# Jobs get TensorE in even steps and VectorE in odd ones, and the scans lie 138 steps behind the attention

## The chip, the cores and the metric

The kernel runs on one core of one Trainium2 chip. Its time is the device time of one execution in microseconds (us); the time given for a kernel is the median of its runs. A core has five engines with queues of their own: TensorE (PE in the profile; PEld is its loading of weights), VectorE (DVE), ScalarE (ACT), GpSimd (POOL) and SyncE (SP), which here only issues DMAs. TensorE writes its results into PSUM[...].

## The reference

Two layers in sequence, on x of 4 images x 128 channels x 64 x 64, all in float32. The first is attention over the 4096 positions of an image, with four heads of 32 channels, a residual and a layer norm:

```python
Q = split_heads(x_flat @ Wq + bq)      # and K, V alike
attn = softmax(einsum('bhnd,bhmd->bhnm', Q, K) * scale, axis=-1)
out = einsum('bhnm,bhmd->bhnd', attn, V)
y = out @ Wo + bo + x_flat
y = layernorm(y) * gamma + beta
```

The second is a sum of three branches on its output:

```python
spatial = conv_3x3(x) + conv_spatial_b
spectral = irfft2(conv_1x1(rfft2(x)))
xi, z = split(u @ in_proj)                   # u: x as 4096 rows; 2 x 256 channels
xs = silu(causal_conv_4_taps(xi))
dt, Bm, Cm = split(xs @ x_proj)              # 8, 16, 16 columns
dt = softplus(dt @ dt_proj + dt_proj_b)
h = exp(dt * A) * h + dt * Bm * xs           # per position; 16 states per channel
y = sum(h * Cm) + xs * D
ym = (y * silu(z)) @ out_proj
return spatial + spectral + ym
```

## The kernel before

**Tiling.** The 4 x 4096 positions are cut into 32 chunks of 512 (`L`), eight per image (`NCH`). The heads are taken in two pairs (`PAIRS`), so a chunk of queries has two halves, 64 in all (`HALVES`). A half goes over the 4096 keys in 32 blocks of 128 (`NT`). One block for one half is a step; a chunk takes 64 steps (`SLOT`), and the attention takes 2,048 steps, counted by `t` from 0. Keys and values of one image stay in SBUF; while one image is worked on, those of the next are projected, one chunk in each period of 64 steps.

**One step.** Nothing is scheduled by a compiler: the loop in lines 1059 to 1107 writes the instructions in the order in which each engine runs them. In a step it issues

- `scores_for_exp(H, m)` (L486): six matmuls (L494) into the PSUM tile "s2", four of queries against keys and two that subtract each query's maximum (`MX`); ACT takes the exponential (L502).
- `scores_for_max`, seven steps ahead (`LEAD`): four matmuls (L454) into the PSUM tile "s1", of which DVE takes the maximum (L461).
- the scans of an earlier chunk. At `LAG` = 144 steps behind the attention each chunk has 2 x 16 pairs of channel half and state, each taking two steps. Even steps issue `scan_state` (L834): the scan itself on DVE (L844), a copy of the last column (L853) and the product with C (L854) on POOL, and the accumulation (L871, L873) on POOL. Odd steps issue `scan_decay` (L827, ACT, into PSUM "dA"), `scan_input_term` (L832, POOL) and, where a buffer is free, `scan_load` (L810 or L816), which SP issues.
- the jobs, by `plan.step` (below).
- `times_values` (L505): four matmuls (L514) that multiply the exponentials with the values. After the last block of a half, the result is copied out of PSUM in two parts, by ACT (L524) and DVE (L525).

"s1", "s2" and "dA" have one buffer each: the matmuls that write one wait until its reader is done.

**Jobs.** All other work is written as generators, `Job`s, in a `Plan` (L84 to L158). A job yields what its next piece needs: "P" for TensorE, "D" for VectorE, "A" for ScalarE, "B" for one of two PSUM banks, "" for nothing but the next step. `plan.step(t, places)` goes over the open jobs by rank, start time and age, and advances each of them whose needs the step's places hold; a place is used up by each advance. After its first advance a job goes on in the same step only over yields that are just "P" (late: "P", "A" or "D") and have a place; any other yield waits for a later step. POOL instructions and DMAs need no place: they are issued with the piece that they stand in. A job that can't have what it needs waits for a later step, and so do its followers.

The main loop hands out places by step (L1093 to L1104): before the attention's first steps all engines; in the attention, odd steps `{"D": 2, "P": 2, "A": 2}` and even ones `{"D": 0, "P": 0, "A": 1}`, so TensorE and VectorE jobs go into odd steps only; after the attention (`plan.late`) only odd steps, with `{"D": 4, "P": 4, "A": 6}`.

**The jobs in question**, with their start lines L1030 to L1057:

- keys and values of a chunk of the next image: `project_kv` (matmuls L350, L364; DVE L355; ACT L376), queries: `project_q` (L417).
- `maxima` (L463): four DVE operations (L467 to L471) form the maxima of the coming half, TensorE transposes them (L476), ACT copies them out as `MX` (L482), which `scores_for_exp` of that half reads.
- `normalise` (L529), for each finished half: SP stores the sums of the exponentials (L541) and the values (L543), reloads the sums in another layout (L546), DVE takes the reciprocal (L549), SP stores it (L551) and reloads it spread over the rows (L554), POOL multiplies (L558). Then `output_projection` (L567): matmul L573, residual L576 on DVE, transposes L580, layer-norm statistics L587 to L593 on DVE, their logarithm and exponential on ACT (L595, L596), small products on POOL (L598 to L601), normalising on DVE (L610).
- `mamba_input` (L644) and `scan_input` (L683) for each half of the channels: matmuls L661 and L687, the four taps on DVE (L697, L702), a sigmoid (ACT L626 to L636 with one DVE piece, L634), its product on POOL (L712). `scan_bc` (L718) follows with two matmuls (L724), and `scan_dt` (L738; matmul L742, ACT L748 to L760, POOL L765 to L767, ACT L774).
- `gate` (L777; matmul L783, a sigmoid, POOL L791), `spectral` (L887; L893, L903, L905), `convolve` (L917; nine matmuls L928 and one L933, ACT L938), `scan_output` (L961; the gate's product, matmuls L995, DVE L999, flipped rows on POOL, L958 and L959), `flips` (L1007), which finishes chunks of an image's first half once the flipped rows are there.

**After the attention.** The last chunk's scans end well over a hundred steps behind its attention; in them the accumulation goes to TensorE (L880, `add_states`, four steps after the scan) instead of POOL, in four buffers taken from the values' space. The two score tiles, and the values' PSUM tile, are used again there.

Of the kernel before, what the change touches and what calls it, by code (L numbers as in the profile page):

```python
# [17 lines left out]
P = 128  # L18
# [143 lines left out]
def attention_then_conv_mamba(  # L162
# [164 lines left out]
    plan = Plan(2, {"x": 2, "f": 1})  # L327
# [114 lines left out]
    def scores_for_max(H, s):  # L442

        k = H % PAIRS
        m, t = divmod(s, TPC)
        assert have["K", k, m] == H // PAIRS // NCH
        if s == 0:
            part[H] = att.tile([P, TPC, 2, NCH], F32, tag="part", name=f"part_{H}")

        tag = "s2" if H == 0 and s % 2 else "s1"  # L450
        sc = psum.tile([P, 2, L], F32, tag=tag, name=f"s1_{H}_{s}")
        for n in range(2):
            for j in range(2):
                nc.tensor.matmul(  # L454
                    sc[:, j, :],
                    QT[H][rows[j], n, t * P : (t + 1) * P],
                    KK[k][m][rows[j], :],
                    start=n == 0,
                    stop=n == 1,
                )  # L460
        nc.vector.tensor_reduce(part[H][:, t, :, m], sc, AX.X, ALU.max)  # L461
# [24 lines left out]
    def scores_for_exp(H, m):  # L486

        k = H % PAIRS
        i, t = divmod(m, TPC)
        assert have["K", k, i] == H // PAIRS // NCH  # L490
        s = psum.tile([P, 2, L], F32, tag="s2", name=f"s2_{H}_{m}")
        for n, mov in enumerate((QT[H][:, 0, :], QT[H][:, 1, :], MX[H])):
            for j in range(2):
                nc.tensor.matmul(  # L494
                    s[:, j, :],
                    sel[rows[j], :] if n == 2 else KK[k][i][rows[j], t * P : (t + 1) * P],
                    mov[rows[j], :],
                    start=n == 0,
                    stop=n == 2,
                )  # L500
        e = att.tile([P, 2, L], F32, tag="e", name=f"e_{H}_{m}", bufs=3)
        nc.scalar.activation(e, s, AF.Exp)  # L502
        es[H, m] = e
# [273 lines left out]
    def gate(c):  # L777

        gates[c] = [None, None]
        for hf in range(NH):  # L780
            bank = yield "PB"
            pz = bank_tile(bank, [P, RPC, W], f"pz_{c}_{hf}")
            nc.tensor.matmul(  # L783
                pz, inw[:, DI + hf * P : DI + (hf + 1) * P], inner(c), start=True, stop=True
            )
            yield "A"
            plan.release(bank)
            z = loc.tile([P, L], F32, tag=f"zg{hf}", name=f"zg_{c}_{hf}", bufs=1)
            nc.scalar.activation(z, pz.rearrange("p r w -> p (r w)"), AF.Identity)
            a = yield from sigmoid(z, "sgz", f"{c}_z{hf}")  # L790
            nc.gpsimd.tensor_tensor(z, z, a, ALU.mult)  # L791
            gates[c][hf] = z
# [28 lines left out]
    def scan_decay(c, v):  # L821
        n, hf = divmod(v, NH)
        k = hf * NS + n

        tag = "o" if plan.t >= HALVES * NT + 2 and v % 2 else "dA"
        dA[c, v] = psum.tile([P, L], F32, tag=tag, name=f"dA_{c}_{k}")
        nc.scalar.activation(dA[c, v], dts[c][hf], AF.Exp, scale=negA[:, k : k + 1])  # L827
# [89 lines left out]
    def convolve(c):  # L917

        i = c % NCH
        while c not in edges or c not in hxs:  # L920
            yield ""
        bank = yield "PB"
        pf = bank_tile(bank, [P, RPC, W], f"pf_{c}")
        for k in range(9):
            if k:
                yield "P"
            dy, dx = divmod(k, 3)
            nc.tensor.matmul(  # L928
                pf, cw[:, k, :], xps[c][:, dy : dy + RPC, dx : dx + W], start=k == 0, stop=False
            )  # L930
        flat = pf.rearrange("p r w -> p (r w)")
        yield "P"
        nc.tensor.matmul(flat, g_hil, hxs.pop(c), start=False, stop=True)  # L933
        yield "A"
        plan.release(bank)
        ym = loc.tile([P, L], F32, tag="ym", name=f"ym_{c}", bufs=2)
        yms[c] = ym
        nc.scalar.activation(ym, flat, AF.Identity, bias=col("conv_b"))  # L938
        if i == 0:
            nc.gpsimd.tensor_tensor(ym[:, :W], ym[:, :W], sbias, ALU.add)  # L940
# [20 lines left out]
    def scan_output(c):  # L961

        b, i = divmod(c, NCH)
        late = i < NCH // 2
        yield "f"
        while not all(gates[c]) or c not in yms:
            yield ""

        for hf in range(NH):
            if c in sums_late:  # L970
                total = sums_late[c][:, hf, :]
                if (c, hf) in accs:
                    nc.vector.tensor_tensor(accs[c, hf], accs[c, hf], total, ALU.add)
                    total = accs[c, hf]
                else:
                    accs[c, hf] = loc.tile([P, L], F32, tag=f"acc{hf}", name=f"acc_{c}_{hf}")
                nc.vector.tensor_tensor(accs[c, hf], total, gates[c][hf], ALU.mult)
            else:
                nc.gpsimd.tensor_tensor(accs[c, hf], accs[c, hf], gates[c][hf], ALU.mult)
        if not late:  # L980
            wr = load_flipped(c)
        for _ in range(3):
            yield ""
        bank = yield "PB"
        pf = bank_tile(bank, [P, L], f"py1_{c}")
        for hf in range(NH):
            if hf:
                yield "P"
            nc.tensor.matmul(
                pf, outw[:, hf, :], accs[c, hf], start=hf == 0, stop=hf == NH - 1  # L990
            )
        yield "D"
        plan.release(bank, 2)
        ob = loc.tile([P, L], F32, tag="ob", name=f"ob_{c}", bufs=1)
        nc.vector.tensor_tensor(ob, yms.pop(c), pf, ALU.add)  # L995
        if late:
            yield ""
            ymd[c] = dram.tile([P, L], F32, tag="ymd", name=f"ymd_{c}", bufs=NCH)
            nc.sync.dma_start(ymd[c], ob)  # L999
        else:  # L1000
            add_flipped(ob, wr)
            yield ""
            yield ""
            nc.sync.dma_start(out[b, :, i * L : (i + 1) * L], ob)
        plan.places["f"] += 1
# [19 lines left out]

    LEAD = 7
    SLOT = PAIRS * NT
    LAG = 2 * SLOT + 16
    STATES = NH * NS
    for b in range(B):  # L1030

# [16 lines left out]
    for c in range(CHUNKS):  # L1048
# [3 lines left out]
        plan.at(t0 + SLOT + 30, 3, convolve(c))  # L1052
        plan.at(c * SLOT + LAG + 6, 3, gate(c))
        plan.at((c + 1) * SLOT + LAG + (2 if c < CHUNKS - 3 else 6), 0, scan_output(c))
    for b in range(B):
# [3 lines left out]
    t = 6 - SLOT  # L1059
    loaded = 0  # L1060
    end = (CHUNKS + 3) * SLOT
    while t < end or not plan.idle():
        H, m = divmod(t, NT)
        if 0 <= H < HALVES:
            scores_for_exp(H, m)
        h1, s1 = divmod(t + LEAD, NT)
        if 0 <= h1 + 1 < HALVES:
            scores_for_max(h1 + 1, s1)
        H, m = divmod(t - 1, NT)
        last = m == NT - 1  # L1070
        if last and 0 <= H < HALVES:
            times_values(H, m)
        c, s = divmod(t - LAG, SLOT)
        odd = s % 2 == 1
        if -1 <= c < CHUNKS:
            v = c * STATES + s // 2
            if not odd:
                if v >= 0:
                    scan_state(*divmod(v, STATES))
            else:  # L1080
                if 0 <= v + 1 < CHUNKS * STATES:
                    scan_decay(*divmod(v + 1, STATES))
                if 0 <= v + 2 < CHUNKS * STATES:
                    late = t > HALVES * NT
                    scan_input_term(
                        *divmod(v + 2, STATES), nc.vector if late else nc.gpsimd
                    )

                if loaded < CHUNKS * NS and loaded // NS in bcds:
                    if ring[0] or spare and spare[0][0] <= t:  # L1090
                        scan_load(*divmod(loaded, NS))
                        loaded += 1
        plan.late = t > HALVES * NT  # L1093
        if plan.late:
            add_states()
            if odd:
                plan.step(t, {"D": 4, "P": 4, "A": 6})
            plan.t = t
        elif t < -LEAD:
            plan.step(t, {"D": 4, "P": 4, "A": 4})  # L1100
        elif odd:
            plan.step(t, {"D": 2, "P": 2, "A": 2})
        else:
            plan.step(t, {"D": 0, "P": 0, "A": 1})  # L1104
        if not last and 0 <= H < HALVES:
            times_values(H, m)
        t += 1
# [76 lines left out]
```

## Time and the profile before

| what | value |
|---|---|
| median of 3 runs | 6037.3 us (6036.54 to 6038.84) |
| profiled execution, own time | 6038.33 us |
| its span | 6036.5 us |
| TensorE clock granted, mean | 0.987 |
| maxima L461: DVE, 2048 times | mean 1221 ns |
| exponentials L502: ACT, 2048 times | mean 1023 ns |
| scans L844, with a state carried in: DVE, 826 times | mean 1275 ns |
| products L854, POOL, 948 times | mean 1277 ns |
| input terms L832, POOL, 948 times | mean 1282 ns |
| accumulations L873, POOL, 894 times | mean 1281 ns |

The span is the part of the execution from the first to the last recorded instruction. A line of the page's groups has: line, engine, operation, output<-inputs, partitions x elements, count; then busy time and the mean of one in ns; then the idle time of the engine just before such instructions and what ended most of it. A line of the waits view has: the waiting group <- what released it, then the sum of the waits in us, their count, and the longest. A line of the timeline has: start and duration in us, engine, line, operation, output<-inputs, sizes and number of equal instructions in a row, and in brackets the idle time before it with its releaser. Where the text says "opening", it means the first matmuls L494 of a step.

### The profile page before, as it was taken

How to read it: one execution, taken by the hardware profiler on the slowest of the kernel's cores; microseconds unless marked ns; L12 is line 12 of the kernel's file. 1: busy time of each engine (PE TensorE's matmuls, PEld its weight loads, DVE VectorE, ACT ScalarE, POOL GpSimd, SP SyncE). 2: the span in 40 equal slices, each digit the busy share in tenths (PEclk: the TensorE clock that was granted, in tenths of full speed). 3: DMA queues.
4: the chain of work that ended last, by engine and by line, in shares of the span. 5: the costliest groups of instructions: out<-in, count | busy, mean ns of one | idle time of the engine just before them, and what ended most of it. 6: DMA issues, size and time to landing. Idle time of an engine off the chain costs nothing. (4 is left out here: it accounts for less than half of the span.)

```text
span 6036.5 us, 82731 instructions
## 1 busy us (share of the span) xinstructions
PE 5847.1 (97%) x31382; PEld 2443.1 (40%) x31382; DVE 4360.0 (72%) x4569; ACT 3586.6 (59%) x4826; POOL 4482.6 (74%) x4522
## 2 busy tenths in 40 slices
PE   5999999999999999999999999999999999999976
PEld 2444444444444444444444444444444444444422
DVE  4557777777777777777777777777777777777657
ACT  1455666666666666666666666666666666666653
POOL 0006888778887778888788888777888887888877
PEclk7999999999999999999999999999999999999988
DMA  4012222224333223223432222322433222222233
GB/s 125 25 36 58 65 71 75 71 70 110 82 89 73 73 72 74 72 64 89 104 84 82 74 68 71 75 68 73 108 75 92 67 67 63 66 71 63 62 98 89
DMA packets 266641, 455.28 MB, mean 75 GB/s; under 512 B 46688, under 2 KB 48256, under 8 KB 266240
## 3 DMA queue, kind: packets, MB, share of 16 engines
q1 hardware_dynamic: 261584, 448.11, 28.1%
q8 instruction: 246, 4.03, 0.3%
q10 hardware_dynamic: 4656, 1.87, 0.1%
q14 instruction: 155, 1.27, 0.1%
HBM read 375.68 MB, written 65.80 MB: 73 GB/s over the span
## 5 line engine op out<-in xcount | busy, mean ns | idle before, releaser
L461 DVE TENSOR_REDUCE part<-s 128x2 f32<-128x1024 f32 x2048 | 2498.1, 1221 | 1411.4 <-PE s L454 1407.6
L502 ACT ACTIVATE e<-s 128x1024 f32<-128x1024 f32 x2048 | 2095.5, 1023 | 2121.6 <-PE s L494 2117.0
L514 PE MATMUL po<-e,V 128*33 128x512 f32 x8192 | 2180.9, 605 | 2.4 <-DVE oz L525 0.3
L494 PE MATMUL s<-Q,K 64*128 64x512 f32 x8192 | 1501.0, 444 | 13.5 <-ACT e L502 10.2
L454 PE MATMUL s<-K,Q 64*128 64x512 f32 x8192 | 1308.9, 397 | 41.4 <-DVE part L461 32.3
L854 POOL TENSOR_TENSOR hs<-hs,bc 128x512 f32<-128x512 f32 x948 | 1211.0, 1277 | 170.3 <-DVE hs L844 101.3
L494 PEld LDWEIGHTS s<-Q,K 64*128 64x128 f32 x8192 | 610.2, 185 | 1736.3 <-ACT e L502 1237.0
L832 POOL TENSOR_TENSOR db<-u,bc 128x512 f32<-128x512 f32 x948 | 1215.6, 1282 | 0.0
L873 POOL TENSOR_TENSOR acc<-acc,hs 128x512 f32<-128x512 f32 x894 | 1145.4, 1281 | 70.1
L844 DVE TENSOR_TENSOR_SCAN hs<-dA,state,db 128x512 f32<-128x512 f32 x826 | 1052.8, 1275 | 41.9 <-ACT dA L827 40.1
L454 PEld LDWEIGHTS s<-K,Q 64*128 64x128 f32 x8192 | 750.1, 185 | 294.9 <-DVE part L461 129.4
L494 PE MATMUL s<-MX,sel 64*128 64x512 f32 x4096 | 808.0, 391 | 0.0
L827 ACT ACTIVATE dA<-dt,negA 128x512 f32<-128x512 f32 x1024 | 703.2, 687 | 115.7 <-DVE V L844 69.5
L853 POOL COPY state<-hs 128x1 f32<-128x1 f32 x858 | 157.9, 184 | 789.8 <-DVE hs L844 786.0
L514 PEld LDWEIGHTS po<-e,V 128*33 128x33 f32 x8192 | 305.4, 109 | 886.5 <-issue 840.8
L494 PEld LDWEIGHTS s<-MX,sel 64*128 64x128 f32 x4096 | 383.9, 185 | 90.7
L928 PE MATMUL pf<-xp,cw 128*128 128x512 f32 x576 | 288.2, 618 | 0.0
L558 POOL TENSOR_TENSOR op<-op,rz 128x512 f32<-128x512 f32 x32 | 41.4, 1294 | 178.6 <-DMA rz<-rd 175.8
L844 DVE TENSOR_TENSOR_SCAN hs<-dA,zero,db 128x512 f32<-128x512 f32 x128 | 163.2, 1275 | 0.9 <-POOL db L832 0.7
L880 PE MATMUL acc<-V,cst 128*128 128x512 f32 x140 | 95.0, 783 | 63.6 <-POOL V L854 63.5
L928 PEld LDWEIGHTS pf<-xp,cw 128*128 128x128 f32 x576 | 96.8, 189 | 119.6 <-issue 117.9
L712 POOL TENSOR_TENSOR xs<-xs,sg_x 128x512 f32<-128x512 f32 x64 | 81.8, 1279 | 79.3 <-ACT sg_x L636 79.3
(147 smaller groups left out, 3571.2 us busy)
## 6 DMA issues: line engine op xcount, KB each, us to landing
bc<-bcd SPq DMA_DIRECT2D x487, 512.0 KB
Q<-qd SPq DMA_DIRECT2D x256, 128.0 KB
K<-kd SPq DMA_DIRECT2D x64, 256.0 KB
K<-bcd SPq DMA_DIRECT2D x42, 256.0 KB
vd<-vst SPq DMA_DIRECT2D x32, 264.0 KB
V<-vd SPq DMA_DIRECT2D x32, 264.0 KB
xq<-in_x SPq DMA_DIRECT2D x32, 256.0 KB
xk<-in_x SPq DMA_DIRECT2D x32, 256.0 KB
```

The source lines that it names most:

```text
L454: nc.tensor.matmul(sc[:, j, :], QT[H][rows[j], n, t * P : (t + 1) * P], KK[k][m][rows[j], :], start=n == 0, stop=n == 1,)
L461: nc.vector.tensor_reduce(part[H][:, t, :, m], sc, AX.X, ALU.max)
L494: nc.tensor.matmul(s[:, j, :], sel[rows[j], :] if n == 2 else KK[k][i][rows[j], t * P : (t + 1) * P], mov[rows[j], :], start=n == 0, stop= ...
L502: nc.scalar.activation(e, s, AF.Exp)
L514: nc.tensor.matmul(po[H][used[j], :], VA[i][:, t, 2 * k + j, :], e[:, j, :], start=m == 0, stop=m == NT - 1,)
L827: nc.scalar.activation(dA[c, v], dts[c][hf], AF.Exp, scale=negA[:, k : k + 1])
L832: engine.tensor_tensor(db[c, v], us[c][hf], bcs[c, n][0], ALU.mult)
L844: nc.vector.tensor_tensor_scan(hs, dA.pop((c, v)), db.pop((c, v)), state[:, k : k + 1] if c % NCH else zero, ALU.mult, ALU.add,)
L853: nc.gpsimd.tensor_copy(state[:, k : k + 1], hs[:, L - 1 :])
L854: nc.gpsimd.tensor_tensor(hs, hs, bcs[c, n][1], ALU.mult)
L873: nc.gpsimd.tensor_tensor(accs[c, hf], accs[c, hf], hs, ALU.add)
L928: nc.tensor.matmul(pf, cw[:, k, :], xps[c][:, dy : dy + RPC, dx : dx + W], start=k == 0, stop=False)
```

## The change

Two things are changed. `LAG` goes from 144 to 138, so that everything that is placed by it comes six steps earlier against the attention: the scans of every chunk with their loads, decays and input terms, and the start times of `gate` and `scan_output`. And the places for jobs are split by step. In the attention, odd steps keep two for VectorE and two for ScalarE and lose TensorE's two, which go to the even steps. After the attention, VectorE's four stay in odd steps, TensorE's four go to even steps, and ScalarE's six are three in each. `plan.t = t` after `plan.step` in the late part goes too: since `plan.step` is now called in every step and sets it, it is set after `add_states` instead of in every step by a line of its own. The places before the attention's first steps stay.

```diff
@@ -1025,7 +1025,7 @@
     LEAD = 7
     SLOT = PAIRS * NT
-    LAG = 2 * SLOT + 16
+    LAG = 2 * SLOT + 10
@@ -1094,14 +1094,15 @@
         if plan.late:
             add_states()
             if odd:
-                plan.step(t, {"D": 4, "P": 4, "A": 6})
-            plan.t = t
+                plan.step(t, {"D": 4, "P": 0, "A": 3})
+            else:
+                plan.step(t, {"D": 0, "P": 4, "A": 3})
         elif t < -LEAD:
             plan.step(t, {"D": 4, "P": 4, "A": 4})
         elif odd:
-            plan.step(t, {"D": 2, "P": 2, "A": 2})
+            plan.step(t, {"D": 2, "P": 0, "A": 2})
         else:
-            plan.step(t, {"D": 0, "P": 0, "A": 1})
+            plan.step(t, {"D": 0, "P": 2, "A": 1})
```

## The prediction

> **What bounds the kernel now.** I read the page first, then the waits of TensorE, then the timeline of one period and of the end. The chain that ended last holds only the final 5 us and says nothing here. From the page:
>
> ```profile
> PE 5847.1 (97%) x31382; PEld 2443.1 (40%) x31382; DVE 4360.0 (72%) x4569; ACT 3586.6 (59%) x4826; POOL 4482.6 (74%) x4522
> PE   5999999999999999999999999999999999999976
> POOL 0006888778887778888788888777888887888877
> ```
>
> TensorE is busy in every slice but the first and the last two, so the run has two parts: the attention, bound by TensorE, up to about 5813 us, and an end of some 220 us in which it isn't. In the timeline each step opens with the first scores matmuls for the exponential; here are three openings in a row:
>
> ```profile
> 5689.86 0.73 PE L494 MATMUL s<-Q,K 64*128 64x512 f32 x4
> ...
> 5692.20 0.73 PE L494 MATMUL s<-Q,K 64*128 64x512 f32 x4
> ...
> 5694.54 0.73 PE L494 MATMUL s<-Q,K 64*128 64x512 f32 x4
> ```
>
> A step without anything else takes 2.344 us, and of the 2,048 openings most stand exactly so far apart, or that plus the TensorE job in the step. No plan can shorten these, only the stalls. The waits view names them:
>
> ```profile
> PE acc L880 <- POOL V L854: 63.5, 38, 14.9
> ...
> PE s L454 <- DVE part L461: 32.3, 62, 1.5
> ...
> PE s L494 <- ACT e L502: 10.2, 44, 1.4
> ```
>
> The first is in the end; the other two, 42.5 us, are most of what the attention loses. The scores' two PSUM tiles have one buffer each, so a late maximum (DVE) or exponential (ACT) stops TensorE. The largest recurs once in each 64-step period:
>
> ```profile
> 2516.91 0.69 DVE L525 COPY oz<-po 33x512 f32<-33x512 f32 x1 [0.38 <-ACT oz L524]
> ...
> 2517.64 1.28 DVE L844 TENSOR_TENSOR_SCAN hs<-dA,state,db 128x512 f32<-128x512 f32 x1
> ...
> 2518.84 1.20 DVE L461 TENSOR_REDUCE part<-s 128x2 f32<-128x1024 f32 x1
> ...
> 2520.09 0.73 PE L454 MATMUL s<-K,Q 64*128 64x512 f32 x4 [0.47 <-DVE part L461]
> ```
>
> The copy of a finished half and a scan come before the maximum, and TensorE waits. The start-to-start spacings in this view give effective costs: exponential 0.92, decay 0.61, another ACT job about 0.6; maximum 1.15, scan 1.20, DVE job 0.66. In a bare step an exponential may be 0.26 us late and a maximum 0.37 us before TensorE feels it.
>
> **What the Trainium skill says.** "PSUM — Partial Sum Buffer", Engine vs sequencer instructions: the queues of ScalarE, VectorE and GpSimd are strict FIFO. The trace agrees: the maximum above stands behind copy and scan though its scores ended at 2517.60. "SBUF — State Buffer" (section on the engine and DMA sides): a DVE operation with two SBUF inputs and a GpSimd operation exclude each other. It agrees: L471 on 128x8 takes 159 ns at the least and 1264 in the median, the length of a POOL product, so the four operations of `maxima` last 1.96 us. "Perfetto Trace Analysis", Identifying the Most-Contended Engine, warns that matmul busy time doesn't measure headroom; hence I count openings of steps.
>
> **The change, part by part.** The order of both programs shows what moves: 607 of 608 groups of TensorE jobs stand in even steps (before, all 598 in odd ones), DVE jobs stay in odd ones. ACT jobs keep their places, but follow sooner.
>
> 1. *TensorE work.* A job alone costs 1.06 us and a pair of the same 1.91, so a group costs 0.20 beside its matmuls. Ten more groups are 2.0 us; four convolution matmuls (three L928, one L933) come in before the attention's end instead of after it, 4 x 0.86 = 3.4. Sum +5.4.
>
> 2. *Stalls that go*, per period, read as the excess over 2.344 by position in the period (22 full periods with a key/value job): 0.31 at 21 (layer-norm statistics, then ACT waits; now followed by L989's 1.91 us of TensorE), 0.27 and 0.10 at 10 and 11 (L417, L774, then L634), 0.14 at 33 and a share of the 0.93 at 34 (five ACT jobs at the half's boundary, now four steps earlier), 0.08 at 52. Two are inside job steps: L661 with L783 takes 1.83 where its matmuls need 1.45 (as L476 with L928), and L364 takes 1.51 for what L893 does in about 1.12: 0.38 and 0.39. All: 2.60 us.
>
> 3. *Stalls that stay or come.* The odd half's boundary: the copy, the scan and the maximum are unchanged, 0.78; now two DVE jobs follow in each of the next odd steps with no TensorE job until ten steps on: 0.12 + 0.10 + 0.08, so 1.08. The key step (L355, L356, L634): 0.31, no longer hidden. Two odd steps with two ACT jobs and a bare step after them (0.92 + 0.61 + 1.2 = 2.73 against 2.344 + 0.26): 0.11 each, as the same load shows before. Two new waits: MX of the even half is copied by ACT (L482) one step before the scores that read it, not four; exponential, decay and copy end 3.13 us after that step's opening and the MX matmul is due at 2.344 + 0.57 = 2.91, so 0.28 with the semaphore. And `scan_bc` (L724) comes two steps behind POOL's product L712, not three. POOL's queue there, in the same constellation of before:
>
> ```profile
> 2556.24 1.29 POOL L873 TENSOR_TENSOR acc<-acc,hs 128x512 f32<-128x512 f32 x1
> 2557.49 1.28 POOL L712 TENSOR_TENSOR xs<-xs,sg_x 128x512 f32<-128x512 f32 x1
> ```
>
> It ends 7.36 us after the scores for the maximum of its own step (2551.41); L724's second matmul is due 7.0 us after (two steps, the key stall, L364 and the first matmul): 0.42. Behind it on TensorE stand the values matmuls and so all that follows. Sum 2.31, so -0.29 x 22 = -6.4. The last eight periods have no key jobs: before 1.96 + 0.38, after 1.08 + 0.11 + 0.11 + 0.28 and 0.90 at the even boundary, where L933 no longer stands: +0.14 x 8 = +1.1. Together -5.3. A bound: if no new wait forms, -23; if each is twice as long, about +13.
>
> 4. *The end.* Three scans fewer are left at the attention's end (69, not 72). There a state takes 1.92 us (scan to scan, DVE alone). More matters what delays it:
>
> ```profile
> 5830.06 0.39 SPq L810 DMA_DIRECT2D bc<-bcd  x1
> ...
> 5830.54 0.41 SPq L546 DMA_DIRECT2D zc<-zd  x1
> ...
> 5835.19 0.20 DVE L549 RECIPROCAL zc<-zc 128x8 f32<-128x8 f32 x1 [6.28 <-DMA zc<-zd]
> ...
> 5845.48 0.75 DVE L576 SCALAR_TENSOR_TENSOR xr<-pa,bo,xr 128x512 f32<-128x512 f32 x1 [2.41 <-PE pa L573]
> ```
>
> SP's queue is stuck behind a load that waits for POOL to free its buffer (POOL's product of 5828.32), so the sums' reload, the reciprocal and the last output projection come late: L576 ends 33.7 us after the last opening (5812.56), with 64 scans left. In the new order the reload has no such load between it and its stores; the reciprocal comes after three scans and POOL's L558 right behind two products. POOL's own queue (L765 to L767 twice and seven products) then ends L558 some 20 us after the last opening, L576 at 22, with 62 scans left: 11.7 + 2 x 1.92 = 15.5 us. Given back: one scan less of cover before L731 (1.9) and loads of the flipped rows two steps nearer their reader (0.6, from nothing to 5 as the longest wait of this kind in the end). Net -13, between -20 and -2.
>
> SP's other work moves with its steps; the state loads keep their distance to the scans (nine steps), so I cost them at nothing; POOL, 81% busy in a period, is their cover.
>
> Sum: +5.4 - 5.3 - 13 = -12.9 on the profiled execution's 6038.3, so 6025.4; its 1.0 us over the median taken off, 6024.
>
> **The rivals.** *The new waits don't form* (POOL and ACT run earlier than I place them): 0.70 x 22 + 0.28 x 8 = 17.6 off, 6007. For it: ACT is 59% busy; against: the spacings are measured. *The end gives it back* (POOL waits for the flipped rows and stops the four V buffers): 6037, no change; two waits of scans for PE in the end, 3.4 and 5.0 us, are of this kind. *Slower*: L712. Each 0.1 us that POOL is later costs 2.2 us; one more product ahead of it (1.28 us, say a backlog from the accumulations) costs 28: 6052. It undoes the gain from 0.59 us and is slower beyond noise from 1.14. POOL's 81% speaks for it; against, its queue is idle 1.2 us shortly before.
>
> **How the numbers follow.** 0.2% is 12 us, about what the measurement can tell from no change. Forecast 0.47 (own range 6010 to 6037; 0.29 of it faster, 0.18 the same), no waits 0.25, end given back 0.14, POOL late 0.14. Faster 0.54, same 0.32, slower 0.14. The range takes in both bounds of the stalls: 5998 to 6050.
>
> **What would show it.** Right: waits of scores on maxima at about the same sum, those at 21 and 11 gone; a wait of L494 on ACT's MX at even halves; L724 waiting on L712; reciprocal near 12 us after the last opening, and L576 10 us earlier. Wrong: TensorE's openings shifted by DVE or POOL in steps not named here, or the end as long as now.

## The result, and the profile after

The changed kernel takes 6072.4 us in the median (6071.26 to 6073.56), the kernel before 6038.07 us beside it: a ratio of 1.0055, interval 1.0044 to 1.0065. It is slower by 0.55%, where 6024 us and at most 6050 were forecast.

The two profiled executions differ by 33.0 us in span (6069.5 against 6036.5). By the openings of the steps:

| stretch, us | before | after | forecast of the difference |
|---|---|---|---|
| to the first opening | 128.5 | 127.8 | 0 |
| first to last opening (the attention) | 5684.1 | 5719.8 | +0.1 |
| last opening to the end | 224.0 | 221.8 | -13 |

So the attention lost 35.7 us, and the end gave back 2.1. The waits of TensorE after (what waited, what released it, sum in us, times, longest):

```profile
PE acc L880 <- POOL V L854: 70.8, 38, 17.2
PE s L454 <- DVE part L461: 45.1, 96, 1.5
...
PE s L494 <- ACT MX L482: 4.9, 28, 0.4
PE pd L724 <- POOL xs L712: 4.0, 19, 0.2
PE s L494 <- ACT e L502: 3.9, 13, 0.8
```

Waits for the exponential went from 10.2 to 3.9 us, the two waits that were named as new (MX, L712) are there, and the wait for the maximum, which was to keep its sum, rose from 32.3 to 45.1. These sums see only part of the loss: a wait that falls on a load of weights has a line of its own (PEld), and the stall of 0.61 us shown below appears as 0.34. Openings see all of it. I took each step's length, less the 2.344 us of a bare step, less its TensorE jobs (0.20 us for a group, that is, for all jobs that stand in one step, 0.855 for a matmul of 128 x 512, less for the narrower ones); what is left I call its excess, and the position is the step's number in its period of 64. The same measure is used for both kernels and for all experiments. Mean excess in the 22 full periods with a key job:

| position | before | after | the prediction had for after |
|---|---|---|---|
| 0, 2, 6 (boundary of the even half) | 0 | 0.41, 0.13, 0.17 | 0.28, 0.11, 0.11 |
| 10, 11 | 0.37 | 0 | 0 |
| 21 | 0.31 | 0 | 0 |
| 27 | 0.45 (in a job step) | 0.56 (a bare step) | nothing |
| 33 to 37 (boundary of the odd half) | 1.06 | 1.11 | 1.08 |
| 47 (key step) | 0.41 | 0.37 | 0.31 |
| 48 (L364, L724) | 0 | 0.57 | 0.42 |
| all 64 | 2.93 | 3.63 | 2.31 |

By these costs the TensorE jobs make +9.1 us, the excess of these 22 periods +15.4 and that of the last eight +11.4. (The first two periods hold up to 3 us that change from kernel to kernel.)

The largest line that the prediction doesn't have is position 27. The timeline of VectorE in period 10, before (positions 25 to 28):

```profile
1954.17 1.23 DVE L461 TENSOR_REDUCE part<-s 128x2 f32<-128x1024 f32 x1
1955.31 1.36 DVE L610 TENSOR_SCALAR xh<-py,mv,r 128x128 f32<-128x128 f32 x4
1956.58 0.68 DVE L995 TENSOR_TENSOR ob<-ym,py 128x512 f32<-128x512 f32 x1
1957.18 1.22 DVE L461 TENSOR_REDUCE part<-s 128x2 f32<-128x1024 f32 x1
...
1959.50 1.21 DVE L461 TENSOR_REDUCE part<-s 128x2 f32<-128x1024 f32 x1
1960.62 0.21 DVE L467 TENSOR_REDUCE mx<-part 128x8 f32<-128x64 f32 x1
...
1963.03 1.23 DVE L461 TENSOR_REDUCE part<-s 128x2 f32<-128x1024 f32 x1 [0.30 <-PE s L454]
```

And after (positions 24 to 26):

```profile
1957.38 1.27 DVE L844 TENSOR_TENSOR_SCAN hs<-dA,zero,db 128x512 f32<-128x512 f32 x1
1959.16 1.23 DVE L461 TENSOR_REDUCE part<-s 128x2 f32<-128x1024 f32 x1 [0.51 <-PE s L454]
1960.30 0.21 DVE L467 TENSOR_REDUCE mx<-part 128x8 f32<-128x64 f32 x1
1960.54 1.10 DVE L469 TENSOR_SCALAR mhi<-mx 128x8 fp32r<-128x8 f32 x1
1961.68 1.19 DVE L470 COPY wide<-mhi 128x8 f32<-128x8 f32 x1
1962.79 0.16 DVE L471 SCALAR_TENSOR_TENSOR wide<-mx,mhi 128x8 f32<-128x8 f32 x1
1962.87 0.67 DVE L634 SCALAR_TENSOR_TENSOR sg_z<-zg,ln_z 128x512 f32<-128x512 f32 x1
1963.46 1.21 DVE L461 TENSOR_REDUCE part<-s 128x2 f32<-128x1024 f32 x1
1964.60 1.27 DVE L844 TENSOR_TENSOR_SCAN hs<-dA,zero,db 128x512 f32<-128x512 f32 x1
```

The four operations of `maxima` take 2.6 us, since L469 and L470, on 128 x 8, last 1.1 and 1.2. Right behind them stands an L634. It belongs to `gate`, whose start is `LAG` + 6: with `LAG` its start moved six steps, and this L634 from position 53 to 25. And the maxima themselves moved. Their start time is position 25 in both kernels, but before, L610 and L995 held both of VectorE's places there and the maxima came at 27, beside TensorE's L661 and L783; now L610 and L995 stand earlier (21 and 17), and at 25 the maxima meet L634. The maximum of the next step, position 26, whose scores were done at 1961.5, starts only at 1963.46, and the scores of position 27 wait for it. TensorE meanwhile:

```profile
1963.42 0.73 PE L494 MATMUL s<-Q,K 64*128 64x512 f32 x4
1964.00 0.39 PE L494 MATMUL s<-MX,sel 64*128 64x512 f32 x2
1964.73 0.73 PE L454 MATMUL s<-K,Q 64*128 64x512 f32 x4 [0.34 <-DVE part L461]
1965.39 1.05 PE L514 MATMUL po<-e,V 128*33 128x512 f32 x4
1966.37 0.73 PE L494 MATMUL s<-Q,K 64*128 64x512 f32 x4
```

From 1963.42 to 1966.37 are 2.95 us for a step without a job, 0.61 too much. The bracket shows 0.34 of it. (The 0.45 of position 27 before stand behind the pair of L610 and L995 at 25.)

In the end, the reload L546 leaves SP's queue in time, as forecast. The next reload doesn't. SP's queue after, around it:

```profile
5854.29 0.53 SPq L546 DMA_DIRECT2D zc<-zd  x1
5860.54 0.35 SPq L551 DMA_DIRECT2D rd<-zc  x1
5867.94 0.37 SPq L810 DMA_DIRECT2D bc<-bcd  x1
5868.40 0.88 SPq L554 DMA_DIRECT2D rz<-rd  x2
```

The load L810 waits for POOL to free its buffer, and L554 stands behind it: 7.9 us between L551 and L554. The reciprocal comes 12.7 us after the last opening (before 22.6, forecast about 12), but L558 at 26.2 (29.9, forecast 20) and the residual L576 at 32.8 (32.9, forecast 22).

### The profile page after: what moved, and what is told of

The parts are those of the page before. It is cut to its first block, busy times and chain, and to the rows that moved or that the text cites. A ratio compares the mean times of both kernels' runs of the same rounds, so it can differ in the third digit from the quotient of the medians.

```text
span 6069.5 us, 82683 instructions
## 1 busy us (share of the span) xinstructions
PE 5860.9 (97%) x31376; PEld 2431.2 (40%) x31376; DVE 4391.0 (72%) x4566; ACT 3563.7 (59%) x4826; POOL 4491.8 (74%) x4528
## 5 line engine op out<-in xcount | busy, mean ns | idle before, releaser
L514 PE MATMUL po<-e,V 128*33 128x512 f32 x8192 | 2175.5, 605 | 2.6 <-DVE oz L525 0.2
L494 PE MATMUL s<-Q,K 64*128 64x512 f32 x8192 | 1501.3, 444 | 10.2 <-ACT e L502 3.9
L454 PE MATMUL s<-K,Q 64*128 64x512 f32 x8192 | 1308.1, 397 | 49.3 <-DVE part L461 45.1
L832 POOL TENSOR_TENSOR db<-u,bc 128x512 f32<-128x512 f32 x951 | 1220.9, 1284 | 0.0
L873 POOL TENSOR_TENSOR acc<-acc,hs 128x512 f32<-128x512 f32 x897 | 1148.8, 1281 | 70.3
L514 PEld LDWEIGHTS po<-e,V 128*33 128x33 f32 x8192 | 303.6, 109 | 910.5 <-issue 888.0
L928 PE MATMUL pf<-xp,cw 128*128 128x512 f32 x576 | 290.0, 619 | 0.1
L558 POOL TENSOR_TENSOR op<-op,rz 128x512 f32<-128x512 f32 x32 | 40.9, 1278 | 203.7 <-DMA rz<-rd 179.4
L880 PE MATMUL acc<-V,cst 128*128 128x512 f32 x134 | 93.0, 798 | 70.9 <-POOL V L854 70.8
L928 PEld LDWEIGHTS pf<-xp,cw 128*128 128x128 f32 x576 | 96.6, 189 | 115.1 <-issue 103.8
L712 POOL TENSOR_TENSOR xs<-xs,sg_x 128x512 f32<-128x512 f32 x64 | 81.4, 1271 | 69.8 <-ACT sg_x L636 69.8
```

The costliest lines, as they stand in the source:

```text
L454: nc.tensor.matmul(sc[:, j, :], QT[H][rows[j], n, t * P : (t + 1) * P], KK[k][m][rows[j], :], start=n == 0, stop=n == 1,)
L494: nc.tensor.matmul(s[:, j, :], sel[rows[j], :] if n == 2 else KK[k][i][rows[j], t * P : (t + 1) * P], mov[rows[j], :], start=n == 0, stop= ...
L514: nc.tensor.matmul(po[H][used[j], :], VA[i][:, t, 2 * k + j, :], e[:, j, :], start=m == 0, stop=m == NT - 1,)
L832: engine.tensor_tensor(db[c, v], us[c][hf], bcs[c, n][0], ALU.mult)
L873: nc.gpsimd.tensor_tensor(accs[c, hf], accs[c, hf], hs, ALU.add)
L928: nc.tensor.matmul(pf, cw[:, k, :], xps[c][:, dy : dy + RPC, dx : dx + W], start=k == 0, stop=False)
```

## The experiments

All ratios are to the kernel before, with their intervals; the last two columns are from the profiled execution.

| kernel | ratio | attention, us | end, us |
|---|---|---|---|
| before | 1 | 5684.1 | 224.0 |
| the change | 1.0055 (1.0044 to 1.0065) | 5719.8 | 221.8 |
| e1_lag140 | 1.0087 (1.0073 to 1.01) | 5743.6 | 217.7 |
| e2_places_only | 1.001 (1.0003 to 1.0017) | 5689.0 | 225.7 |
| e3_one_d | 1.0029 (1.0017 to 1.0041) | 5701.7 | 222.8 |
| e4_hold | 1.0046 (1.0033 to 1.0058) | 5721.4 | 215.8 |
| e5_d1_three | 1.0017 (1.001 to 1.0023) | 5696.3 | 221.5 |
| e6_d1_three_hold | 1.0008 (1.0002 to 1.0015) | 5698.1 | 217.0 |
| e7_bc_later | 1.0052 (1.0039 to 1.0064) | 5721.7 | 219.7 |
| e8_lag140_one_d | 1.0019 (1.0012 to 1.0027) | 5704.2 | 215.2 |
| e9_late_only | 1.0003 (0.9994 to 1.0011) | 5684.2 | 224.6 |
| e10_late_hold | 1.0001 (0.9992 to 1.0009) | 5684.1 | 224.2 |
| e11_best | 1.0006 (0.9997 to 1.0014) | 5687.6 | 226.5 |

**Shift or places?** The old places with a shift of four steps, and the new places without a shift.

```diff
-    LAG = 2 * SLOT + 16
+    LAG = 2 * SLOT + 12        # e1, in the kernel before
```

> The kernel before with the scans 140 steps behind (138 needs loads of B and C that the old places don't have ready yet), TensorE and VectorE jobs still together in odd steps. Theory S (split): it is the places that cost; VectorE's jobs now stand in bare steps of 2.34 us, where before they stood beside a TensorE job that lengthened the step and hid them. Then this one stays at 6030 to 6040 us, with the last opening at about 5813. Theory C (collision): the cost comes with the shift, because gate() now falls on the maxima; here the maxima share their step with L610 at position 25. Then the attention is 10 us or more longer than before, 6045 or above.

```diff
-    LAG = 2 * SLOT + 10
+    LAG = 2 * SLOT + 16        # e2, in the changed kernel
```

> The new places with the scans 144 steps behind as before. Theory S: nearly all of the 35.7 us that the attention lost stays, last opening at 5840 or later, about 6070 us. Theory C: no L634 beside the maxima, so at least the 0.56 us of position 27 go in each period (18 us of 32): last opening at 5830 or before, about 6055 us. In its order position 27 has six pieces of scan_input on ScalarE instead of three; if these stop TensorE as the collision did, 27 keeps a stall of 0.5 us for another reason, by the exponential (L502) and not by the maximum (L461).

e1 is the slowest kernel of all, with 59.5 us more attention, and e2 loses 4.9 us. Theory S falls in both. The new places alone give an excess of 2.65 us a period (before 2.93), 6 us less in the 22 periods; +4.0 of TensorE jobs and some 7 in the last eight periods make up the +4.9. So of the 35.7 us some 5 come with the places alone and some 31 when the shift is added to them. The two don't simply add up: under the old places a shift of only four steps costs 59.5. Position 27 has no excess at all in e2, though six pieces of `scan_input` stand on ScalarE there: that fear was idle. Instead 0.69 shows at position 2, behind the boundary of the even half, where no TensorE job but one L933 stands.

In e1 L995 has left position 25 (it stands at 21), and the maxima take its place there beside L610's four operations. VectorE and then TensorE there:

```profile
1966.30 1.36 DVE L610 TENSOR_SCALAR xh<-py,mv,r 128x128 f32<-128x128 f32 x4
1967.58 0.21 DVE L467 TENSOR_REDUCE mx<-part 128x8 f32<-128x64 f32 x1
1967.82 0.87 DVE L469 TENSOR_SCALAR mhi<-mx 128x8 fp32r<-128x8 f32 x1
1968.73 1.20 DVE L470 COPY wide<-mhi 128x8 f32<-128x8 f32 x1
...
1969.91 1.21 DVE L461 TENSOR_REDUCE part<-s 128x2 f32<-128x1024 f32 x1
```

```profile
1971.18 1.04 PE L454 MATMUL s<-K,Q 64*128 64x512 f32 x4 [1.84 <-DVE part L461]
```

The maximum, whose scores were done at about 1967.5, starts 2.4 us later; TensorE waits 1.84 us in one go, and position 27 has an excess of 1.79 a period.

**Taking the maxima apart from the rest**, in the changed kernel and in e1:

```diff
-            plan.step(t, {"D": 2, "P": 0, "A": 2})
+            plan.step(t, {"D": 1 if t % NT == NT - LEAD else 2, "P": 0, "A": 2})   # e3
-            plan.step(t, {"D": 2, "P": 2, "A": 2})
+            plan.step(t, {"D": 1 if t % NT == NT - LEAD else 2, "P": 2, "A": 2})   # e8, in e1
```

> The changed kernel with one place for VectorE instead of two in the step of the maxima, so that L634 of gate() comes two steps later; nothing else moves. Theory C: position 27 loses its 0.56 us, minus at most 0.1 for L634 in the next odd step: 13 to 18 us off, about 6056 us. Theory S: L634 costs about the same in any bare step, so at most 5 us off, 6067 or above.

> The old places with the scans 140 steps behind (e1, 6091 us) and one place for VectorE in the step of the maxima, which puts them two steps behind L610 again, as in the kernel before. If their standing together was the cost of e1: 1.3 us at position 27 and 0.5 at 30 go in each period, 50 us off, 6040 to 6050. If the shift costs in another way, 6070 or above.

In e3, L634 comes two steps later and nothing else moves. VectorE:

```profile
1959.14 0.16 DVE L471 SCALAR_TENSOR_TENSOR wide<-mx,mhi 128x8 f32<-128x8 f32 x1
1959.22 1.21 DVE L461 TENSOR_REDUCE part<-s 128x2 f32<-128x1024 f32 x1
1960.35 1.27 DVE L844 TENSOR_TENSOR_SCAN hs<-dA,zero,db 128x512 f32<-128x512 f32 x1
1961.54 1.20 DVE L461 TENSOR_REDUCE part<-s 128x2 f32<-128x1024 f32 x1
1962.65 0.67 DVE L634 SCALAR_TENSOR_TENSOR sg_z<-zg,ln_z 128x512 f32<-128x512 f32 x1
```

The maxima are as slow as before, but the maximum follows them directly, and L634 costs nothing in the next odd step. Position 27 falls from 0.56 to below 0.03, all other positions but 53 (0.08, now under 0.03) keep their values to within 0.02, and the attention is 18.1 us shorter. e8, where the maxima stand at 27 again, takes 39.3 us from e1. So 18 of the change's 36 us are shown to be this meeting, and the same happens with other work under other places. Of the 17.6 us that e3 still has over the kernel before, about 9 are TensorE jobs, about 8 lie in the last eight periods and less than 2 in the 22 before them; what causes those of the last eight wasn't followed.

**The pair of the key step and L724.**

```diff
-            plan.step(t, {"D": 2, "P": 0, "A": 2})
+            plan.step(t, {"D": 1 if t % SLOT in (25, 45, 57) else 2, "P": 0, "A": 2})   # e5
```

> The changed kernel with one place for VectorE at positions 25, 45 and 57 of a period of 64 steps (maxima twice, and the key step, where L356 and an L634 stood together). In its order L634 comes at 27 and 47, L724 two steps later, away from L364 but still two steps behind L712; L476 comes at 60 instead of 62, so MX is copied three steps before its reader. Theory P (pairs of VectorE work in a bare step stop the next maximum): 0.56 at 27, 0.37 at 47 and the 0.41 at position 0 go, 1.3 us a period or 40 us in all, about 6030 us. The L712 rival of the prediction: then 0.4 to 0.6 us stay at 50, where L724 now is; if that stall belonged to the pair as well it goes too, and 6020 us follows.

```diff
         if len(xss[c]) == NH:
+            yield ""
+            yield ""
             plan.now(1, scan_bc(c))                                                # e7
```

> The changed kernel with scan_bc two steps later, so that L724 stands four steps behind L712 and no longer beside L364; the VectorE pair at 45 stays. If L724 waits for POOL's L712: the 0.57 us of position 48 go (but for what L364 itself has), 47 keeps 0.37, about 12 us off, 6060. If the 0.57 are the stall of L364 behind the pair at 45, they stay at 48: under 5 us off. L928 moves later by a step pair, so position 0 and 2 may change by 0.1 to 0.4 either way.

e5 is 23.6 us shorter in the attention, not 40. The three stalls do go: positions 27, 47 and 0 are empty, and TensorE's waits for MX fall from 28 to 7. But 0.2 to 0.3 us each come at 4, 8 and 9 (an L634 now meets L418 in step 7), and the shifted jobs fall into 628 TensorE groups instead of 607, 4 us more. At 50, where L724 now is, 0.54 stays, but the smaller part of it for L712: the waits view has two such waits in the whole execution (1.6 us), and in most other periods the third L724 starts 0.54 us after the second instead of 0.43, in all some 0.2 a period. The larger part, 0.33, comes with the L903 that now follows L724 in the step (more on that in the last section); in e7 below, L724 stands in front of another matmul of 128 rows (L905) and waits for nothing, and position 50 has just these 0.33.

L712 is the prediction's rival for a slowdown. In the changed kernel it is really there. POOL, then TensorE:

```profile
2020.62 1.27 POOL L873 TENSOR_TENSOR acc<-acc,hs 128x512 f32<-128x512 f32 x1
2021.85 1.26 POOL L712 TENSOR_TENSOR xs<-xs,sg_x 128x512 f32<-128x512 f32 x1
```

```profile
2020.79 1.16 PE L364 MATMUL pv<-wat_vo,xk 128*128 128x128 f32 x8
2021.88 1.07 PE L724 MATMUL pd<-xs,xpw 128*64 128x512 f32 x2
2023.17 0.64 PE L724 MATMUL pd<-xs,xpw 128*64 128x512 f32 x1 [0.22 <-POOL xs L712]
2023.18 1.05 PE L514 MATMUL po<-e,V 128*33 128x512 f32 x2
2023.65 0.59 PE L724 MATMUL pd<-xs,xpw 128*64 128x512 f32 x1
```

The third L724 starts 0.05 us after L712's end, and so it does in all 21 periods in which L724 stands beside L364. In 19 of them it comes 0.79 to 0.82 us after the second, where 0.43 separate the two when nothing is waited for. So the wait is a part of the 0.57, some 0.37, and 7 us in all; the waits view has 4.0. e7 removes the wait, and position 48 falls to 0.01. The 0.71 of the even boundary fall to 0.05 as well. But the attention is no shorter (+1.9): 0.61 comes at position 52, where the copies of `scan_bc` and L911 stand with the decay on ScalarE, and TensorE's waits for the exponential rise from 3.9 to 16.2 us; 0.33 comes at 50, and 0.33 at 4 and 8 together. My expectation of 12 us off was wrong, and so was the other reading, that L364 kept the stall: other places took it.

**The end.**

```diff
-                    if ring[0] or spare and spare[0][0] <= t:
+                    if not HALVES * NT < t < HALVES * NT + 8 and (
+                        ring[0] or spare and spare[0][0] <= t
+                    ):                                                             # e4
```

> The changed kernel with the one scan load that stands between L551 and L554 of the last half held back until after L554. If SP's queue is what delays the last projection: L554 is issued at about 13.5 us after the last opening instead of 20.8, L558 right behind POOL's products at 19 to 22 instead of 26.2, L576 at 24 to 28 instead of 32.8. If the end is then bound by the scans alone, it is 4 to 9 us shorter (215 us from last opening to the end instead of 222), about 6065 us. If the end is bound by POOL and the four V buffers, the projection comes earlier and the end stays within 2 us.

> The kernel of the run before with the scan load held back as in e4: the attention as there, the end 6 us shorter, as e4 showed (216 us for 222), if the two are independent. About 6024 us; faster than the kernel before the change.

In e4 SP's queue around the reload is

```profile
5864.04 0.35 SPq L551 DMA_DIRECT2D rd<-zc  x1
5865.48 0.78 SPq L554 DMA_DIRECT2D rz<-rd  x2
5871.43 8.43 SPq L810 DMA_DIRECT2D bc<-bcd  x2
```

L554 is out 14.3 us after the last opening (5851.15), L576 at 27.0 instead of 32.8, and the end is 6.0 us shorter. e6 repeats it with e5's attention, by 4.5 us. It was expected to be faster than the kernel before and isn't, because its attention is 14.0 us longer than before's.

> The kernel before with the change's places after the attention alone (144 steps, old places in the attention). The attention must stay at 5684 us between the first and the last opening. The prediction's reason for the end was the reload L546 leaving SP's queue earlier: here it does, but a scan load stands before L551. If that load blocks as L810 did in the changed kernel, the reciprocal comes earlier and the last projection does not: end 224 us, time 6038, no change. If the new late places are worth something of themselves, the end is 5 us or more shorter.

> The run before with that load held back until after L554. As in e4, L554 is issued right after L551 and the end is about 6 us shorter: 218 us, 6032 us, faster than the kernel before. If the gain of e4 needed the shorter distance, the end stays at 224.

e9 is the kernel before with only the changed lines under `if plan.late`; e10 adds e4's edit. The attention stays at 5684.2 and 5684.1 us. In e9 L576 comes at 29.8, in e10 at 28.7 after the last opening instead of 32.9, and the end is as long as before in both. With 144 steps and the new places, 65 scans are left behind L576 instead of before's 64, and from L576 to the end e10 takes 195.5 us where before takes 191.0: what L576 wins is given back there. e10's expectation failed. The hold itself moves L576 by only 1.2 us in e10, where it was 5.9 in e4: L554 is out 7.3 us earlier than in e9, but L558, which there stands behind POOL's products, starts only 0.7 us earlier.

The old places after the attention do better with a shorter distance. e1 and e8 have them, with 140 steps; L576 comes at 31.7 and 30.7, 62 scans are left behind it as in the changed kernel, and the end takes 217.7 and 215.2 us, without a hold. One thing that the new places cost can be read in e4, POOL's queue and then TensorE's:

```profile
5873.30 1.27 POOL L558 TENSOR_TENSOR op<-op,rz 128x512 f32<-128x512 f32 x1
5874.51 0.18 POOL L853 COPY state<-V 128x1 f32<-128x1 f32 x1
5874.77 1.26 POOL L854 TENSOR_TENSOR V<-V,K 128x512 f32<-128x512 f32 x1
```

```profile
5876.09 1.13 PE L880 MATMUL acc<-V,cst 128*128 128x512 f32 x2 [0.63 <-POOL V L854]
5877.06 1.02 PE L573 MATMUL pa<-op,wat_vo 128*128 128x512 f32 x2
```

L573 could start at the end of L558, 5874.57. But an L880 stands in front of it and waits for the product that POOL makes after L558, so it starts 2.5 us later. In the three kernels with the old places there (before, e1, e8) no L880 comes between, and L576 ends 2.0 to 2.9 us after L558; in all others one does, and it takes 4.3 to 6.1.

> The run before with one place for VectorE at position 45, as in e5, in the old places of the attention: L634 comes two steps later and no longer stands beside L356. Theory P: the 0.41 us of L364 at position 47 go in the 22 periods with a key job, 9 us off, about 6023 us. Against it: L731 now stands beside the maxima at 57; there TensorE has 1.9 us of jobs in the same step and in the next ones, which should hide it. If a TensorE job in the same step doesn't hide such a pair, 0.5 us come at 57 to 59 in each period and the time is 6030 or above.

e11 is e10 with one place for VectorE at position 45. The 0.41 at 47 goes, as in e5, and so does the 0.37 at 10 and 11; but the 0.31 at 21 grows to 0.58, 0.1 each comes at 8 and 16, and 0.32 at 55, where L724 now has an L928 behind it. The attention is 3.5 us longer. No kernel tried is faster than the one before.

## Why the prediction was wrong

- **Step 3, stalls that stay or come, is the one that failed.** Its list had 2.31 us a period and 3.63 came. Of the 1.32 between them, 0.33 were there before too, in small stalls that neither list names (2.93 against the 2.60 of step 2); the miss is 0.99 a period, a rise of 0.70 where a fall of 0.29 was forecast, 22 us of the 36 that the attention came out too long. 0.56 of it is position 27, which isn't on the list. The step looked for pairs of VectorE jobs only at the boundary and in the key step, and for TensorE's groups elsewhere; it said itself that the maxima last 1.96 us, but not in which step they stand and what stands beside them once `gate` and L995 come earlier. e3 settles this one: 18 us, the last eight periods included.
- The other misses of that step are sizes: MX 0.41 for 0.28, L724 0.57 for 0.42 (of which the wait for L712 itself is 0.37), the key step 0.37 for 0.31, the steps with two ScalarE jobs 0.30 for 0.22. All lie on the same side. In the last eight periods the rise was +1.43 us for +0.14: 0.47 again at 27 (0.29 before), 0.43 at 0, 0.26 at 48, and 0.23 and 0.17 at 8 and 60, which the prediction didn't name.
- **Step 2, stalls that go,** was right in kind: 10, 11 and 21 are empty.
- **Step 1, TensorE work,** +5.4, measured +9.1. The ten groups (607 for 597) and four convolution matmuls are as counted. Most of the rest is L742, whose two matmuls now mostly stand in two steps in the late periods (18 such steps, before 2); a lone one costs 0.42 beside an L928 instead of 0.23 as one of two, 3 us in all.
- **Step 4, the end,** -13, measured -2.1. "In the new order the reload has no such load between it and its stores" held for L546; the second reload, L554, had one. e4 prices this at 6 us. The remaining 5 are in the projection behind it: with L554 freed, e4's L558 ends 23.4 us after the last opening where the step had 20, and L576 ends 4.3 us after that, not 2, with the L880 in front of L573. The two scans fewer behind L576 gave 2.1 us, about what the step had for them (3.8 less the 2.5 given back). Why L558 comes 3.4 us late wasn't followed.
- **The rivals.** L712 was the one on the slower side and named a real wait, of 0.37 us a period. That is about what the forecast had for it anyway (0.42), so it isn't why the kernel is slower: the rival had 0.14 of the chance and the wrong reason for the sign.
- The Trainium skill, "SBUF — State Buffer", section Who interferes with whom, says more than the prediction took from it: copies and tensor_scalar between SBUF operands can take the port pair that VectorE shares with GpSimd too, not only operations with two SBUF inputs. The trace agrees: L469, a tensor_scalar on 128 x 8, takes 171 ns at the least and 1246 at the most, 321 in the median before and 1026 after, while L471 falls from 1264 to 165. The wait moved from L471 to it. In the lines above L469 and L470 end at 1961.65 and 1962.88; POOL's operations beside them, L873 and L832, end at 1961.62 and 1962.85.

## What to carry to other kernels

When a distance between two pipelines in one step loop is changed, list by position what now stands together on every engine, above all in the steps that hold the longest runs of one job. Look also for jobs that move because another one freed their place, as the maxima did. A job that costs nothing in one step cost 18 us here two steps earlier. A place count by step is a coarse tool: it counts a run of four operations and one of 0.67 us alike. And when one DMA is freed from a load that blocks its queue, look at the next DMA of the same chain.

## What the runs showed of the hardware

Three kernels with the same attention (before, e9, e10) have 5684.1, 5684.2 and 5684.1 us between first and last opening, while single runs of them lie between 6036.5 and 6044.4 us: for questions within one stage the openings tell more than the times. And matmuls with few output rows can lie beside each other: in the lines above the values' L514 (33 rows) starts at 2023.18 while two L724 (64 rows) are still to finish. That makes the price of a matmul depend on what follows it. In the kernel before, a step with L724 alone, the values behind it, takes 1.73 us more than a bare step, 0.20 of it for the group: 1.53 for its four passes. In nine steps of the changed kernel an L928 (128 rows) follows instead, and it starts 1.86 us after the first pass of L724; such a step takes up to 2.91 us more than a bare one, and a step with one matmul of L928's size alone 1.05.
